# Output writes of a two-pair scan kernel, issued between the columns' steps, with the last two blocks written separately and the first pair's rows kept off a turn

## The chip, the cores and the metric

The kernel runs on one core of one Trainium2 chip. The metric is the device time of one execution in microseconds; the time of the kernel before is the median of three runs. The profile comes from one more execution, recorded by the hardware profiler, and its times count from the start of its span.

Engines are named as in the profile: PE is TensorE's matrix multiplication and PEld its weight load, DVE is VectorE, ACT is ScalarE, POOL is GpSimd, SP is the engine that issues nearly all the DMAs of this kernel (SPq in the profile). A line such as L1310 is a line of the kernel before.

## What is computed

The input is four images of 48 channels and 256 x 256 pixels in float32. Four layers follow one another, each as `x = x + layer(groupnorm(x))`. Layers 0 and 1 are an attention over channels and a gated convolution; the change does not touch them. Layers 2 and 3 are four scans each, and they fill most of the time:

```python
def step(w, b):                       # one row or column after the other
    def f(carry, inp):
        nxt = inp + _conv1d(carry, w, b)      # 48 -> 48 channels, 5 taps
        return (nxt, nxt)
    return f
# down over the rows, up over the rows, right over the columns, left over the columns
...
x = x + _L3_conv_ref(_gn(x), ...)
```

Every step needs the step before it, so a scan of 256 rows or columns is a chain of 256 convolutions.

## The kernel before

**Pairs and chains.** The four images are two pairs; a pair is one chain, `chain(pair)`, a Python generator that yields after every step of a row or column. In SBUF the 96 partitions hold 48 channels twice (even and odd positions), so the five taps become three matmuls of 96 x 96 by 128 (L1045, in `step`). Each step is done for the two images of the pair one after the other, called half steps below: three matmuls into PSUM, an addition on VectorE into one of four carry tiles (L1049 for the rows, L1053 for the columns), and `after`, which keeps the result: ScalarE's copy with the bias in the down, up and right scans (L1127, L1168, L1248), GpSimd's addition of the layer's input in the left scan (L1289, L1293).

**How the chains are interleaved.** The first chain gets a lead of `LEAD` = 992 steps. Then both chains step in turn, and TensorE has the other pair's matmuls to do while one pair waits for its addition. When the first chain has ended, the second runs its last 992 steps alone: the down, up, right and left scans of layer 3. During those, `to_rows(0)` brings the first pair's result, which lies column-wise in HBM, into the row order of the output: per piece four reads `oi<-x` (L1369) of 768 KB, eight copies in SBUF, six on GpSimd (L1383) and two on ScalarE (L1385), and two writes `out<-oo` (L1387) of 1536 KB. It is a generator of 24 pieces (eight times a set of reads and two halves), and the final loop takes one after every 28 steps.

**The left scan of the second pair** goes through 16 blocks of 16 columns, from n = 15 down to 0. At the first column of block n the loads for block n - 1 are issued on SP: `lines` (L1279), the right scan's result, and `stage` (L1280), the layer's input, 1536 KB each. Both come from a ring of five buffers of one block each, so `lines` takes the buffer of a `stage` used three blocks earlier, and `stage` that of a `lines` used two blocks earlier: it has to wait until VectorE has read the last column of that one. The second pair's result isn't written column-wise: GpSimd adds `stage` and the new carry straight into `done`, two tiles (one an image) that hold two blocks in row order, 32 columns. They come from the first pair's ring, which is otherwise used by then only for the rows of `to_rows`. After each even block four writes `out<-done` (L1310) go out, two images by two row parities, each of 768 KB in 6144 runs of 32 elements (128 B).

**The turn** is the change from the up scan to the right scan. The first block of columns (`col`) needs the first rows of the up scan (`col<-up`, L1180, and `col<-last`, L1192) directly out of SBUF; the second block is read from HBM (`col<-U`, L1235), after the last writes into `U` (L1200, L1207) have landed.

**What sets the order of the work.** Engines take their instructions in order. The order on each queue follows the order of emission only loosely: a scheduler at build time places each instruction by its own estimate of when its inputs and its buffer are ready, and adds the semaphore waits. In the order that results for the kernel before, SP has, for every two blocks of the left scan, the four writes, then `stage`, `lines`, `stage`, `lines`.

Of the kernel before, what the change touches and what calls it, by code (L numbers as in the profile page):

```python
# [16 lines left out]
B, C, H, W = 4, 48, 256, 256  # L17
# [97 lines left out]
def rows(pair):  # L115
    return slice(pair * P, (pair + 1) * P)
# [848 lines left out]
def scans(ctx, tc, xs, out, wts, biases, dram, k, coefs, lead, spare):  # L965
# [13 lines left out]
    nc = tc.nc  # L979
# [19 lines left out]
    CB = 2 * KC  # L999
# [12 lines left out]
    def take(pair, name):  # L1012
        return buffers[pair].tile([P, SLOT], F32, tag="slot", name=name)

    def chain(pair):
# [8 lines left out]
        def slot(name):  # L1024
            return take(pair, f"{name}{pair}")

        def inner():
            return carry[at[0]][:, :, 1 : HP - 1]
# [27 lines left out]
        def rows_view(t):  # L1056
            return t.rearrange("p (b k h w) -> p b k h w", b=2, k=NK, w=KC)

        def cols_view(t):
            return t.rearrange("p (b q h w) -> p b q h w", b=2, q=2, w=KC)  # L1060

        def lines_view(t):

            return t.rearrange("p (w b h) -> p w b h", w=CB, b=2)

        def row(ts, r):
            return rows_view(ts[r % 2])[:, :, :, r // 2, :]

        def load_rows(layer, n, ts, k0, k1):

            for r in range(2):
                v = rows_view(ts[r])
                for q in range(2):
                    for b in range(2):
                        nc.sync.dma_start(
                            v[q * C : (q + 1) * C, b, k0:k1].rearrange("c k h w -> c k (h w)"),
                            xs[layer][pair][
                                r * C : (r + 1) * C, b, 2 * k0 + q : 2 * k1 - 1 + q : 2, n * NH : (n + 1) * NH, :
                            ].rearrange("c k h w -> c k (h w)"),
                        )  # L1080

        def layer_of(layer, first):
# [32 lines left out]
            for n in range(NT):  # L1115
                ahead_ = None
                for r in range(RT):
# [3 lines left out]
                    if ahead_ and r >= RT // 2 and r % 4 == 0:  # L1121
                        i = (r - RT // 2) // 4
# [3 lines left out]
                    def keep(new, b):  # L1126
                        nc.scalar.activation(inp[:, b], blocks(new[:, b]), AF.Identity, bias=bias[:, 0:1])  # L1127
# [15 lines left out]
            for n in reversed(range(NT)):  # L1143
                ahead_ = None
                for r in reversed(range(RT)):
# [16 lines left out]
                    i = n * RT + r + 1  # L1162
                    if i == H:
                        continue
                    place = row(now, r)
# [4 lines left out]
                    if i == H - 1:  # L1170
                        keep(inner(), slice(0, 2))
                    else:
                        step(layer, 0, place, keep)
# [93 lines left out]
            following = None  # L1267


            direct = layer == 1 and pair == NP - 1  # L1270
            done = None
            for n in reversed(range(NK)):
                ahead_ = None
                if direct and n % 2 == 1:
                    done = [take(0, "done") for _ in range(2)]
                for w in reversed(range(CB)):
                    if w == CB - 1 and n > 0:
                        ahead_ = slot("lines"), slot("stage")
                        nc.sync.dma_start(ahead_[0], Rt[n - 1])  # L1279
                        nc.sync.dma_start(by_batch(ahead_[1]), block_of(x, n - 1))  # L1280
                    if layer == 0 and n == 0 and w == CB // 2:
                        following = [slot("dn"), slot("dn")]
                        load_rows(1, 0, following, 1, NK)
                    line = lines_view(lines)[:, w]
                    to = cols_view(stage)[:, :, w % 2, :, w // 2]

                    def keep(new, b):
                        if not direct:
                            nc.gpsimd.tensor_add(to[:, b], to[:, b], new[:, b])  # L1289
                            return  # L1290
                        for i in range(b.start, b.stop):
                            place = done[i].rearrange("p (h w) -> p h w", w=2 * CB)[:, :, n % 2 * CB + w]
                            nc.gpsimd.tensor_add(place, to[:, i], new[:, i])  # L1293

                    if n == NK - 1 and w == CB - 1:
                        keep(inner(), slice(0, 2))
                    else:
                        step(layer, 2, line, keep)
                    if late:
                        late.pop(0)()  # L1300
                    yield
                if not direct:
                    nc.sync.dma_start(block_of(y, n), by_batch(stage))
                elif n % 2 == 0:
                    for b in range(2):
                        at_rows = out[(2 * pair + b) * C : (2 * pair + b + 1) * C].rearrange(
                            "c (h r w) -> c h r w", r=2, w=W
                        )
                        for r in range(2):
                            nc.sync.dma_start(  # L1310
                                at_rows[:, :, r, n * CB : (n + 2) * CB],
                                done[b][r * C : (r + 1) * C].rearrange("c (h w) -> c h w", w=2 * CB),
                            )
                if layer == 0:

                    def stat(b, c, n=n, v=by_batch(stage)):
                        nc.vector.bn_stats(stats[b][:, n * 4 + c, :], v[:, b, c * 512 : (c + 1) * 512])

                    late += [lambda b=b, c=c, f=stat: f(b, c) for b in range(2) for c in range(4)]
                    if n == 0:  # L1320
                        for r in range(2):
                            for q in range(2):
                                nc.sync.dma_start(
                                    rows_view(following[r])[q * C : (q + 1) * C, :, 0].rearrange("c b h w -> c b (h w)"),
                                    cols_view(stage)[r * C : (r + 1) * C, :, q, :NH, :].rearrange("c b h w -> c b (h w)"),
                                )
                if ahead_:
                    lines, stage = ahead_
            if layer == 0:

                ends = []
                for b in range(2):
                    mv = work.tile([P, 2], F32, tag=f"mv{pair}{b}", name="mv")
                    late.append(
                        lambda b=b, mv=mv: nc.vector.bn_aggr(mv, stats[b].rearrange("p a b -> p (a b)"))
                    )
                    ends.append(k.group_norm_pieces(work, p_small, mv, "mean6", coefs[3][2 * pair + b], f"{pair}{b}"))
                for piece in late:
                    piece()
                    yield  # L1340
                for i in range(2):
                    for both in ends:
                        both[i]()
                    yield
                yield following
# [13 lines left out]
    def to_rows(pair):  # L1359

        y = xs[2][pair]
        nh = SLOT // W
        to = out[rows(pair)].rearrange("p (h w) -> p h w", w=W)
        for n in range(H // 2 // nh):
            got = []
            for r in range(2):
                t = take(pair, "oi")
                for b in range(2):
                    nc.sync.dma_start(  # L1369
                        t[b * C : (b + 1) * C].rearrange("c (k n) -> c k n", k=2 * NK),  # L1370
                        y[r * C : (r + 1) * C, b, :, n * nh : (n + 1) * nh, :].rearrange("c k h w -> c k (h w)"),
                    )
                got.append(t.rearrange("p (k q h w) -> p k q h w", k=NK, q=2, w=KC))
            yield
            for half in range(2):
                o = take(pair, "oo")
                v = o.rearrange("p (h r k w q) -> p h r k w q", h=nh // 2, r=2, k=NK, q=2)
                here = slice(half * nh // 2, (half + 1) * nh // 2)
                for i in range(4):
                    r, q = i // 2, i % 2  # L1380
                    dst, src = v[:, :, r, :, :, q], got[r][:, :, q, here, :].rearrange("p k h w -> p h k w")
                    if i < 3:
                        nc.gpsimd.tensor_copy(dst, src)  # L1383
                    else:
                        nc.scalar.copy(dst, src)  # L1385
                h0 = 2 * n * nh + half * nh
                nc.sync.dma_start(to[:, h0 : h0 + nh, :], o.rearrange("p (h w) -> p h w", w=W))  # L1387
                yield
# [9 lines left out]
        next(chains[1])  # L1398

    pieces = to_rows(0)  # L1400
    for i, _ in enumerate(chains[1]):
        if i % 28 == 27:
            next(pieces, None)
    assert next(pieces, True) is True

# [123 lines left out]
```

## Time and profile before

| What | Value |
|---|---|
| median of three runs (9152.1 to 9154.33) | 9154.29 us |
| the profiled execution, its own time | 9152.88 us |
| its span (first to last instruction) | 9151.1 us |
| mean granted TensorE clock | 0.979 |
| busy: PE, PEld, DVE, ACT, POOL | 95%, 80%, 41%, 38%, 23% |
| DMA, whole span | 152 GB/s mean, 1390.61 MB |
| chain by engine | PE 89%, DMA 4%, DVE 3%, ACT 2% |
| second chain alone: down and up scans | about 7555 to 8309 us |
| its right scan, from the turn | 8309 to 8667 us |
| its left scan; writes of its output | from 8667; first write issued at 8729.85 |
| last addition on VectorE; end of the last write's packets | 9120.9; 9149.5 us |

How to read it: the chain of waits goes back from the last instruction, at each step to what released it. A piece named PE there is time in which TensorE set the pace; a piece named DMA is time in which an engine waited for a transfer. An SPq line is the issue of a DMA on SP, with the time it held SP; the landing comes later. In the view by windows, "DMA share" is the mean busy share of the core's sixteen DMA engines (packets that overlap can bring it above 1), and PEclk is the granted clock. The view of the DMA queues gives for a window, behind each queue, its packets, its MB, and the time its packets took as a share of sixteen engines' time in the window.

### The profile page before, as it was taken

What the parts mean: (1) busy time and instruction counts of PE and PEld (TensorE: products, weight loads), DVE (VectorE), ACT (ScalarE), POOL (GpSimd) and SP (SyncE); (2) the same over time, 40 slices, a digit from 0 to 9 for tenths busy, and PEclk for the clock granted to TensorE, in tenths of its full rate; (3) what the DMA queues carried; (4) which work ended last, traced back from release to release, by engine and by line L of the source; (5) the groups of instructions that cost most, each with busy time, mean ns of one, the idle gap of its engine ahead of it and who ended that gap; (6) DMA issues with size and microseconds to landing.
All of it is one profiled execution on the core that took longest, in us unless ns stands there. A gap on an engine that the chain in (4) does not pass through costs nothing.

```text
span 9151.1 us, 162340 instructions
## 1 busy us (share of the span) xinstructions
PE 8728.1 (95%) x62920; PEld 7283.8 (80%) x62920; DVE 3763.0 (41%) x10790; ACT 3489.5 (38%) x7033; POOL 2073.9 (23%) x3855
## 2 busy tenths in 40 slices
PE   6999999999999887999999999999999999999986
PEld 4777777433333346999999999999999999998986
DVE  3232010234555564444455444444445554343432
ACT  0001000123343356755502766665661006665500
POOL 0000000001111120002464000003446772003464
PEclk9999999999999988999999999999999999999998
DMA  7663323468788868665587773656556787888677
GB/s 149 133 132 87 73 63 72 95 138 175 173 182 181 174 156 178 130 141 138 142 218 172 146 159 92 153 130 169 145 161 186 218 220 158 180 183 203 172 153 146
DMA packets 1177350, 1390.61 MB, mean 152 GB/s; under 512 B 261072, under 2 KB 1103568, under 8 KB 1113600
## 3 DMA queue, kind: packets, MB, share of 16 engines
q1 hardware_dynamic: 1176480, 1379.90, 66.5%
q8 instruction: 493, 8.08, 0.4%
q14 instruction: 281, 2.30, 0.1%
q0 software_dynamic: 96, 0.33, 0.0%
HBM read 812.02 MB, written 509.61 MB: 144 GB/s over the span
## 4 chain that ended last, share of the span: by engine, by line
PE 89%; DMA 4%; DVE 3%; ACT 2%; issue 1%; SPq 1%; POOL 1%; DVEq 0%; POOLq 0%; ACTq 0%
PE ps L1045 58%; PE py L581 7%; PE acc L294 5%; PE acc L295 5%; PE acc L296 4%; PE py L590 4%; PE pt L276 1%; DMA stage<-x 1%; DMA tok<-x 1%; PE ph L698 1%; ACT x1n L541 1%; PE pout L868 1%; PE ptok L751 1%; DMA x<-y 1%; DMA sx<-in_x 1%
## 5 line engine op out<-in xcount | busy, mean ns | idle before, releaser
L1045 PE MATMUL ps<-carry,w 96*96 96x128 f32 x48960 | 5505.8, 275 | 135.9 <-DVE carry L1053 89.3
L1045 PEld LDWEIGHTS ps<-carry,w 96*96 96x96 f32 x48960 | 5456.1, 163 | 188.9 <-DVE carry L1053 100.5
L1225 POOL COPY pre<-col 96x256 f32<-96x256 f32 x1020 | 656.7, 645 | 2737.5 <-DMA col<-last 1948.3
L1248 ACT ACTIVATE lines<-carry,b 96x128 f32<-96x128 f32 (+1 forms) x2044 | 816.9, 402 | 623.6 <-DVE carry L1053 614.5
L1127 ACT ACTIVATE dn<-carry,b 96x128 f32<-96x128 f32 (+1 forms) x2044 | 770.5, 398 | 715.0 <-DVE carry L1049 712.1
L1049 DVE TENSOR_TENSOR carry<-ps,dn 96x128 f32<-96x128 f32 x2280 | 655.2, 288 | 892.9 <-PE ps L1045 803.3
L1053 DVE TENSOR_TENSOR carry<-ps,pre 96x128 f32<-96x128 f32 x2040 | 587.2, 288 | 796.8 <-PE ps L1045 544.0
L1168 ACT ACTIVATE up<-carry,b 96x128 f32<-96x128 f32 x1792 | 718.3, 402 | 481.6 <-DVE carry L1049 480.6
L1053 DVE TENSOR_TENSOR carry<-ps,lines 96x128 f32<-96x128 f32 x2040 | 577.0, 286 | 741.4 <-PE ps L1045 645.4
L1289 POOL TENSOR_TENSOR stage<-stage,carry 96x128 f32<-96x128 f32 (+1 forms) x1533 | 793.1, 521 | 312.3 <-DVE carry L1053 184.2
L1049 DVE TENSOR_TENSOR carry<-ps,up 96x128 f32<-96x128 f32 x1792 | 516.4, 288 | 678.3 <-PE ps L1045 668.9
L581 PE MATMUL py<-x1n,wy 128*96 128x512 f32 x1536 | 700.8, 605 | 30.2 <-ACT x1n L541 27.9
L294 PE MATMUL acc<-xt 128*96 128x288 f32 x2048 | 666.9, 409 | 0.0
L295 PE MATMUL acc<-xs,xt 128*96 128x288 f32 x2048 | 666.9, 407 | 0.0
L581 PEld LDWEIGHTS py<-x1n,wy 128*96 128x96 f32 x1536 | 244.0, 165 | 452.4 <-issue 435.0
L261 ACT ACTIVATE xn<-raw,coef 96x2048 f32<-96x2048 f32 x64 | 133.6, 2094 | 986.9 <-PE pt L276 819.8
L296 PE MATMUL acc<-xt,xs 128*96 128x192 f32 x2048 | 501.7, 327 | 0.0
L279 DVE COPY xt<-pt 128x384 f32<-128x384 f32 x256 | 136.6, 554 | 851.5 <-PE pt L276 650.6
L296 PEld LDWEIGHTS acc<-xt,xs 128*96 128x96 f32 x2048 | 332.2, 165 | 154.4 <-issue 1.5
L295 PEld LDWEIGHTS acc<-xs,xt 128*96 128x96 f32 x2048 | 332.1, 164 | 151.2 <-issue 2.4
L604 DVE TENSOR_TENSOR y<-py,t 96x512 f32<-96x512 f32 x256 | 171.4, 677 | 592.1 <-PE py L590 586.2
L590 PE MATMUL py<-x2n,wy 64*96 64x512 f32 x1536 | 363.0, 601 | 0.0
(179 smaller groups left out, 4843.4 us busy)
## 6 DMA issues: line engine op xcount, KB each, us to landing
stage<-x SPq DMA_DIRECT2D x64, 1536.0 KB
dn<-x SPq DMA_DIRECT2D x240, 384.0 KB
col<-U SPq DMA_DIRECT2D x60, 1536.0 KB
R<-lines SPq DMA_DIRECT2D x60, 1536.0 KB
lines<-R SPq DMA_DIRECT2D x60, 1536.0 KB
D<-dn SPq DMA_DIRECT2D x56, 1536.0 KB
up<-D SPq DMA_DIRECT2D x56, 1536.0 KB
U<-up SPq DMA_DIRECT2D x224, 384.0 KB
```

The costliest lines, as they stand in the source:

```text
L294: nc.tensor.matmul(acc[0], lhsT=xt[:, h + 2, :], rhs=xt[:, here, :], start=first, stop=last)
L295: nc.tensor.matmul(acc[1], lhsT=xt[:, h + 2, :], rhs=xs[:, here, :], start=first, stop=last)
L296: nc.tensor.matmul(acc[2], lhsT=xs[:, h + 2, :], rhs=xt[:, past, :], start=first, stop=last)
L581: nc.tensor.matmul(ps, lhsT=held["w"][0][:, dx], rhs=x1n[:, 2 * c : 2 * c + 2, dx : dx + W], start=dx == 0, stop=False)
L590: nc.tensor.matmul(held["ps"][q + 2 * s], lhsT=held["w"][1][here, dx], rhs=x2n[here, 2 * q : 2 * q + 2, dx : dx + W], start=False, stop=dx ...
L1045: nc.tensor.matmul(ps, lhsT=w_sb[layer][:, way, j, :], rhs=old[:, i, j : j + W // 2], start=j == 0, stop=j == 2)
L1049: nc.vector.tensor_add(new[:, i].rearrange("p (k w) -> p k w", w=KC), ps.rearrange("p (k w) -> p k w", w=KC), inp[:, i])
L1053: nc.vector.tensor_add(new[:, i], ps, inp[:, i])
L1127: nc.scalar.activation(inp[:, b], blocks(new[:, b]), AF.Identity, bias=bias[:, 0:1])
L1168: nc.scalar.activation(place[:, b], blocks(new[:, b]), AF.Identity, bias=bias[:, 1:2])
L1248: nc.scalar.activation(line[:, b], new[:, b], AF.Identity, bias=bias[:, 2:3])
L1289: nc.gpsimd.tensor_add(to[:, b], to[:, b], new[:, b])
```

## The change

The change is in `layer_of` (the left scan of the last layer of the second pair) and in the last loop of `scans`. It has three parts.

1. The four writes of a block pair are no longer issued together. They go into a list, and one is taken out after the steps with `w % 8 == 4`, which is two a block (in the last two blocks after every fourth step, four a block). What is left in the list when the scan ends is issued then.
2. Blocks 1 and 0 are written separately. Their `done` is one tile for both images with 16 columns, so each gives four writes of 6144 runs of 16 elements (64 B) and 384 KB, in place of four writes of 128 B runs for both blocks.
3. The pieces of `to_rows(0)` come after fixed steps: sixteen from step 20 on, every 26 steps (to 410), and eight from step 508 on, every 28 (to 704). None lies between 410 and 508. The up scan ends at about step 480.

The computation itself and all other DMAs are the same. In the order that the scheduler gives to SP now, each block of the left scan has `lines`, `stage`, write, write (the first pair of writes has `stage` between them); after the last `stage` come the last four writes of 128 B runs, then the eight of 64 B runs.

```diff
             direct = layer == 1 and pair == NP - 1
-            done = None
+            done, width = None, 0
+            writes = []
             for n in reversed(range(NK)):
                 ahead_ = None
-                if direct and n % 2 == 1:
-                    done = [take(0, "done") for _ in range(2)]
+                if direct and n < 2:
+                    done, width = take(0, "done").rearrange("p (b n) -> b p n", b=2), CB
+                elif direct and n % 2 == 1:
+                    done, width = [take(0, "done") for _ in range(2)], 2 * CB
...
-                            place = done[i].rearrange("p (h w) -> p h w", w=2 * CB)[:, :, n % 2 * CB + w]
+                            place = done[i].rearrange("p (h w) -> p h w", w=width)[:, :, n * CB % width + w]
                             nc.gpsimd.tensor_add(place, to[:, i], new[:, i])
...
                     if late:
                         late.pop(0)()
+                    if writes and (w % 4 == 0 if n < 2 else w % 8 == 4):
+                        writes.pop(0)()
                     yield
                 if not direct:
                     nc.sync.dma_start(block_of(y, n), by_batch(stage))
-                elif n % 2 == 0:
-                    for b in range(2):
+                elif n * CB % width == 0:
+
+                    def write(b, r, done=done, width=width, w0=n * CB):
                         at_rows = out[(2 * pair + b) * C : (2 * pair + b + 1) * C].rearrange(
                             "c (h r w) -> c h r w", r=2, w=W
                         )
-                        for r in range(2):
-                            nc.sync.dma_start(
-                                at_rows[:, :, r, n * CB : (n + 2) * CB],
-                                done[b][r * C : (r + 1) * C].rearrange("c (h w) -> c h w", w=2 * CB),
-                            )
+                        nc.sync.dma_start(
+                            at_rows[:, :, r, w0 : w0 + width],
+                            done[b][r * C : (r + 1) * C].rearrange("c (h w) -> c h w", w=width),
+                        )
+
+                    writes += [lambda b=b, r=r, f=write: f(b, r) for b in range(2) for r in range(2)]
...
+            for write in writes:
+                write()
...
     pieces = to_rows(0)
+    times = [20 + 26 * i for i in range(16)] + [508 + 28 * i for i in range(8)]
     for i, _ in enumerate(chains[1]):
-        if i % 28 == 27:
+        if i in times:
             next(pieces, None)
```

## The prediction

> **What bounds the kernel now.** I read the page first (chain by line, tenths of the span), then the chain of waits in order of time for the last 400 us, the SP queue's own timeline there, and the DMA view of short windows. The page says TensorE is busy 95% of the span and makes 89% of the chain; what the change touches is the rest. The last pass of the second pair runs from 8667 us, and from 8730 us its output is written. The chain there:
>
> ```profile
> 8739.93 10.68 PE ps L1045 x96
> 8750.61 15.71 DMA stage<-x
> ...
> 8766.45 0.53 POOL done L1293
> ...
> 8767.34 40.46 PE ps L1045 x332
> 8807.80 15.19 DMA stage<-x
> ```
>
> A load of `stage` ends the wait, 15 us long, and again 57 us later; seven such pieces lie before the end. GpSimd (L1293) waits for the load, VectorE and TensorE for GpSimd through the four carry tiles. Why the load is late is on SP:
>
> ```profile
> 8729.85 20.66 SPq L1310 DMA_DIRECT2D out<-done  x4
> 8750.61 5.51 SPq L1280 DMA_DIRECT2D stage<-x  x1
> 8756.16 0.59 SPq L1279 DMA_DIRECT2D lines<-R  x1
> 8756.85 0.56 SPq L1280 DMA_DIRECT2D stage<-x  x1
> 8757.51 0.56 SPq L1279 DMA_DIRECT2D lines<-R  x1
> ```
>
> Four output writes go out back to back at the end of a block pair and hold SP 20.66 us, then hold up the next issue 5.51 more; the loads for two blocks stand behind them. A block is 16 columns of 1.345 us (VectorE's additions in the timeline, at full clock), 21.5 us, so the stage load comes out just when it is needed. But how much is there to win? The stretches between two late loads:
>
> ```profile
> core 0: us, PE busy (x) PEld busy (x) DVE busy (x) ACT busy (x) POOL busy (x), PEclk, DMA share, GB/s
> 8807.80:8862.53 54.73, 44.37 (x378) 44.05 (x377) 18.05 (x63) 0.00 (x0) 31.93 (x64) 0.91 0.89 173
> 8862.53:8918.05 55.52, 45.55 (x391) 45.21 (x390) 18.73 (x65) 0.00 (x0) 33.09 (x66) 0.91 0.88 171
> ```
>
> A block pair takes 55 to 57 us where the columns need 43, and the DMA share is already 0.88. The queue is badly ordered, and it is also nearly full. The three lines below are the DMA view of 8756 to 8786 (the four loads), 8727 to 8757 (the four writes) and 8336 to 8337 (the tiny `U<-last` writes of 32 B runs at the turn):
>
> ```profile
> q1 hardware_dynamic: 1381, 6.38, 94.3%
> ...
> q1 hardware_dynamic: 24648, 3.21, 75.0%
> ...
> q1 hardware_dynamic: 1348, 0.06, 74.3%
> ```
>
> Loads: 0.943 x 30 = 28.3 us of sixteen engines, 7.07 each. Writes: 0.75 x 30 = 22.5 us, 5.62 each, 14.6 ns a packet on one engine (0.75 x 30 x 16 / 24648). Tiny packets: 8.8 ns (0.743 x 16 / 1348 us).
>
> **What the Trainium skill says.** "Perfetto Trace Analysis", DMA Instruction — HWDGE: the slice of a DMA on its issuing engine is descriptor generation, not movement, and the next instruction stands behind it. The trace agrees: the write's cost shows on SP, and partly in the following load's 5.51 us. "DMA: Bandwidth & Descriptors", Queues, rings and completion order: descriptors of one engine's ring are consumed in order. It agrees too: after 8756 us 6.38 MB of loads move in one run, behind the writes. The same page, Specifications: under 512 B a transfer doesn't reach line rate, because of a read-modify-write; Why small descriptors are slow: a fixed overhead per packet. The trace has both sides: 128 B packets at 14.6 ns, tiny ones at 8.8, so the cost falls far less than the bytes.
>
> **The change part by part.** (1) *Writes one by one.* No packet is removed. In the changed kernel's instruction order SP has, for each block, `lines`, `stage`, write, write, in place of four writes and then two of each load, so a stage load has at most the previous block's two writes ahead of it, and no more the whole four. The `done` wait stays on GpSimd and is long met. What queues behind a write on SP now is the next block's pair of loads. Would the old 15 us wait vanish? TensorE runs on about 6 us past a block's end before it stops (8751.4 to 8757), so the load may be 6 us late for nothing. What is late next is the DMA queue itself: a block brings 2 x 7.07 + 2 x 5.62 = 25.4 us of packets against 21.5 us of columns. So I cost this stretch as DMA-bound: from the first write's packets at 8731 us there are 25 loads (13 of `stage`, 12 of `lines`) and 28 writes, 25 x 7.07 + 28 x 5.62 = 334.2 us, to 9065.2. The last stage load ends four writes earlier, at 9042.7, lands about 2 us later; less 6 us of slack the last block begins about 9039 and computing ends at 9060 (now 9121.6). TensorE then loses 9060 - 8730 - 14 x 21.5 = 29 us instead of 91.
>
> Bounds of this: shares above 1 occur where many transfers overlap (1.06 in the loads' 5 us windows), 334.2 / 1.06 = 315, 19 us less. Upwards, elapsed time: the four writes took 26.3 us from 8730.5 with dips between them (6.6 each), the loads 27 (6.75 each): 25 x 6.75 + 28 x 6.6 = 353.6, 19 us more. Loads queued ahead should fill part of the dips, so I take 334.
>
> (2) *The last two blocks by themselves.* The last pair's four writes become eight of as many packets (6144) at 64 B. No row of before shows 64 B. Lower end the tiny packets, 8.8 ns x 384 per engine = 3.4 us; upper end 128 B, 5.6 us; I take the middle, 4.5, an estimate from those two rows. Eight take 36 us, four of them under block 0, where no load is left to be delayed. They cannot start before the 9065 of the earlier writes, so the queue sets the end: 9065.2 + 36 + 1.6 (from the last packets at 9149.5 to the end of the span now) = 9102.8. That is 48 us under the span of 9151.1. Eight at 3.4 or 5.6 make it 9 less or more. The GpSimd additions keep their count and shape (0.52 us against 0.67 us for a half step): nothing.
>
> (3) *No rows near the turn.* The turn, up to right, loses much: 8309.4 to 8389.2 us has 457 matmuls, at the later 8.73 per us 52 us of work in 80. Its chain:
>
> ```profile
> 8310.14 1.09 ACT oo L1385
> ...
> 8314.66 5.04 DMA col<-last
> ...
> 8339.72 15.34 DMA col<-U
> ...
> 8383.83 1.12 POOL oo L1383
> ```
>
> Only little is the rows' doing: ScalarE's copy and the write behind it (8310.1 to 8311.7) hold two `col<-up` issues that were ready, about 2.5 us; and 1.5 MB of rows (`out<-oo`, issued 8337.5) lie ahead of `col<-U`, about 5.5 us. In the new order ScalarE's copies and both writes stand before the turn, but one 0.77 MB read of rows (7.07 / 2 = 3.5 us) still stands ahead of `col<-U`, and two GpSimd copies (1.1 us each) now come into the first block after it, where the 6 us hold-up at 8383 moves to. The rest, the writes of U that must land, stays. Saving 2.5 + 2 less a little: 4 us, between 0 and 8. The earlier rows come every 26 steps instead of 28; ScalarE's order in the down pass, where the waits are its normalizations (6 us a block), keeps its sequence. I take 0.
>
> Sum: 48 + 4 = 52. The profiled execution took 9152.88 (span 9151.1 and 1.8 around it), the median is 9154.29, 1.4 above; 9154.3 - 52 = 9102.
>
> **The rivals.** (a) *The columns set the pace.* If loads and writes mixed overlap better than they did in a row, a block fits into 21.5 us: computing ends at 8730 + 301 = 9031, then four 64 B writes, 18 us, and 3 around them: 9052, 99 us less, and the turn: 9051. For it: whole 50 us windows show a DMA share of 1.17 (7800 to 7850, other shapes). Against: 25.4 must shrink by 15%, and the writes alone never moved above about 147 GB/s. (b) *The dips stay.* A write behind full rings holds SP, so the next loads come out only when the second write is handed over; `R<-lines` at 8345 was held 12.05 us in that way behind a read of rows. Then elapsed times count: 8731 + 353.6 + 8 x 6.2 + 1.6 = 9136, 15 less, with the turn 9135. (c) *The 64 B packets are dear*, a slower kernel: their place is the end, after 9065, with nothing to hide them. It decides from (9151.1 - 1.6 + 4 - 9065.2) / 8 = 11 us a write, 29 ns a packet, twice the 128 B price; at 15 us the end is 9065.2 + 120 + 1.6 = 9187, 36 later, 9186 with the turn. For it: the read-modify-write that the skill names; against: the tiny packets' 8.8 ns, also into HBM.
>
> **How the numbers follow.** DMA-bound 0.70 (9102, own range 9074 to 9124: 19 and 9 down, and 8 to 19 up); columns 0.11 (9051); dips stay 0.15 (9135); dear packets 0.04 (9186). The range 9074 to 9130 leaves out (a), (c) and the upper part of (b), some 0.2. About 0.2% (18 us) is what a measurement of this kernel tells from no change: faster takes 0.70, 0.11 and 0.10 of (b), 0.91; the same, 0.05; slower 0.04.
>
> **What would show it.** On SP, two writes and two loads in turn from 8730, no run of four until the end; stage waits of 2 to 5 us a block after the first three instead of 15 a pair; DMA share near 1 there; computing ending near 9060, the tail some 40 us with eight 64 B writes of about 4.5. Share below 0.9 with waits left means (b), no waits means (a), a tail beyond 90 us means (c). I am wrong elsewhere if the down pass or the turn shifts by over 10 us.

## The result, and the profile after

| | us |
|---|---|
| before, median of 4 runs | 9153.19 (9148.12 to 9154.33) |
| after, median of 4 runs | 9100.12 (9095.42 to 9107.06) |
| ratio | 0.9942, 95% interval 0.9926 to 0.9958 |
| the profiled execution of after | 9095.42, its span 9093.6 |

The change saves some 53 us, and the forecast was 9102. The two spans lie 57.5 us apart. Cut at the same four instructions, the two traces show where that is:

| stretch | before | after | gained |
|---|---|---|---|
| up to the down scan of the second pair's last layer (nothing in it is changed) | 7555.1 | 7551.7 | 3.4 |
| down and up scans | 719.1 | 726.4 | -7.3 |
| turn and right scan, up to the first output write on SP | 455.6 | 449.1 | 6.5 |
| left scan, from that write to the end of the span | 421.25 | 366.4 | 54.9 |

The first line is what two executions differ by anyway: over the ten profiled executions of this document that stretch took 7550.2 to 7559.4 us. The last line is the change's aim; the two between cancel.

**The left scan.** The SP queue's timeline of after, two stretches of it (start, duration, issue):

```profile
8795.02 0.58 SPq L1284 DMA_DIRECT2D stage<-x  x1
8795.65 17.41 SPq L1316 DMA_DIRECT2D out<-done  x2
8813.16 5.59 SPq L1283 DMA_DIRECT2D lines<-R  x1
8818.84 0.58 SPq L1284 DMA_DIRECT2D stage<-x  x1
...
9014.15 0.58 SPq L1284 DMA_DIRECT2D stage<-x  x1
9014.82 71.32 SPq L1316 DMA_DIRECT2D out<-done  x12
```

Two writes and one `lines` load now stand between two `stage` issues; the groups of four are gone. At the end stand twelve writes together: four of 128 B runs and all eight of 64 B runs. From the issue at 8771.09 to that at 9014.15 are ten blocks, 24.3 us each. The columns need 21.5, so something still waits. The chain of waits of after, its pieces in the last 500 us:

```profile
8599.86 267.49 PE ps L1045 x2370
...
8867.35 15.94 DMA stage<-x
...
8884.33 6.95 PE ps L1045 x60
...
8891.67 15.95 DMA stage<-x
...
9008.67 15.55 DMA lines<-R
...
9024.69 22.98 PE ps L1045 x174
```

From 8599.86 the chain is TensorE alone for 267 us, almost six blocks of writing among them; the first late `stage` ends a wait at 8883.3, where before it was at 8766.3. A DMA piece of 16 us is a load's whole way and not the time that an engine stood. That is in GpSimd's waits from 8700 us on (total, times, longest):

```profile
POOL done L1297 <- DMA stage<-x: 46.3, 8, 7.6
```

Before it was 105.6 us in 7 waits, the longest 15.9. Now the DMA queue itself is the limit. The first two lines below are blocks with no wait yet, the third has one, the last is the tail after the last matmuls (a half step, three matmuls in the program, is six records of PE in these counts):

```profile
core 0: us, PE busy (x) PEld busy (x) DVE busy (x) ACT busy (x) POOL busy (x), PEclk, DMA share, GB/s
8795.02:8818.84 23.82, 23.82 (x215) 23.74 (x214) 10.20 (x36) 0.00 (x0) 18.29 (x37) 1.00 1.10 201
8818.84:8843.00 24.16, 24.16 (x218) 24.11 (x217) 10.37 (x36) 0.00 (x0) 18.63 (x37) 1.00 1.04 196
8989.10:9014.15 25.05, 22.51 (x200) 21.97 (x199) 9.43 (x33) 0.00 (x0) 16.21 (x34) 1.00 1.04 190
9048.10:9093.60 45.50, 0.24 (x3) 0.02 (x1) 0.29 (x1) 0.00 (x0) 1.04 (x2) 0.52 0.98 83
```

The share is above 1 in each of the ten blocks (1.03 to 1.10), and in the first of them TensorE is still full: the loads' issues fall behind by 24.3 - 21.5 = 2.8 us a block, at first unseen, since a load comes out a block ahead of its use. The DMA view of the ten blocks and of 9053 to 9092 (packets, MB, share of 16 engines):

```profile
q1 hardware_dynamic: 126367, 47.18, 105.2%
...
q1 hardware_dynamic: 48747, 3.11, 102.3%
```

47.18 MB in 243 us is 194 GB/s, against 171 to 173 in block pairs before. The second line is the 64 B writes: 1.023 x 39 x 16 / 48747 = 13.1 ns a packet, and 39 / 8 = 4.9 us a write.

A wait costs TensorE more than the time in which it stands. The granted clock in three stretches of after, around the last late load, a `lines` that landed at 9024.2 (columns as above):

```profile
9022.00:9024.00 2.00, 0.91 (x9) 0.69 (x7) 0.00 (x0) 0.00 (x0) 0.52 (x1) 1.00 0.97 213
...
9026.00:9028.00 2.00, 2.00 (x12) 1.99 (x11) 0.54 (x2) 0.00 (x0) 0.00 (x0) 0.52 1.02 238
...
9034.00:9036.00 2.00, 2.00 (x20) 1.99 (x19) 0.86 (x3) 0.00 (x0) 1.90 (x5) 1.00 1.00 138
```

TensorE stands for about 2 us, and then the clock is at 0.50 to 0.52 from 9026 to 9032, with 11 or 12 records in 2 us instead of 20. From the first output write to the end of computing PE is busy 319.6 us before and 311.1 after for the same 2685 records; in the run with half of the writes, further down, where the clock stays at 1.00, it is 301.1. So by these figures the lower clock cost some 18 us before and 10 after, beside 72 and 10 us of standing still.

**The down scan**, where 7 us were lost. After's chain there:

```profile
7821.62 39.83 PE ps L1045 x354
...
7864.83 10.73 DMA dn<-x
```

A load of the down pass ends an idle time that before has not. Its issue on SP, before and then after:

```profile
7824.66 22.86 SPq L1075 DMA_DIRECT2D dn<-x  x8
7849.40 0.35 SPq L1387 DMA_DIRECT2D out<-oo  x1
```

```profile
7845.85 0.33 SPq L1397 DMA_DIRECT2D out<-oo  x1
7846.23 0.42 SPq L1136 DMA_DIRECT2D D<-dn  x1
7846.74 22.87 SPq L1075 DMA_DIRECT2D dn<-x  x8
```

With the pieces 26 steps apart a rows write stands ahead of the eight `dn` loads. SP waits 27.2 us there for ScalarE's copies into the write's tile (L1395 of after), and the loads come out 22 us later (7846.74 against 7824.66). The loads themselves are no slower: SP is on them for 22.9 us in both.

### The profile page after: what moved, and what is told of

Its sections match the earlier page's. It is cut to its first block, busy times and chain, and to the rows that moved or that the text cites. A ratio compares the mean times of both kernels' runs of the same rounds, so it can differ in the third digit from the quotient of the medians.

```text
span 9093.6 us, 162344 instructions
## 1 busy us (share of the span) xinstructions
PE 8711.1 (96%) x62920; PEld 7268.3 (80%) x62920; DVE 3759.8 (41%) x10790; ACT 3489.6 (38%) x7033; POOL 2067.0 (23%) x3855
## 4 chain that ended last, share of the span: by engine, by line
PE 88%; DMA 4%; DVE 3%; ACT 1%; issue 1%; SPq 1%; POOL 1%; DVEq 0%; POOLq 0%; ACTq 0%
PE ps L1045 57%; PE py L581 7%; PE acc L294 6%; PE acc L295 5%; PE acc L296 4%; PE py L590 3%; PE pt L276 1%; DMA stage<-x 1%; DMA tok<-x 1%; PE ph L698 1%; PE pout L868 1%; DMA x<-y 1%; PE ptok L751 1%; ACT x1n L541 1%; DMA sx<-in_x 1%
```

## The experiments

Theory: in the left scan the sum of the DMA packets sets the end once SP's order no longer does; the split of the last blocks costs packets at a place where nothing hides them. Rivals: SP's being held by writes is what still counts; the split or the piece steps carry part of the gain. The first four kernels take the parts separately.

**Part 1 alone**: writes one by one, all of 128 B runs, pieces every 28 steps as before. Against the changed kernel:

```diff
-                if direct and n < 2:
-                    done, width = take(0, "done").rearrange("p (b n) -> b p n", b=2), CB
-                elif direct and n % 2 == 1:
+                if direct and n % 2 == 1:
...
-    times = [20 + 26 * i for i in range(16)] + [508 + 28 * i for i in range(8)]
+    times = [27 + 28 * i for i in range(24)]
```

> The writes one by one, alone: 128 B runs to the end, the rows' pieces at their old steps. Theory (the sixteen DMA engines set the pace, so the end is the sum of their packets): the block pace is that of the changed kernel, 24.3 us, and the end is earlier than its by the eight 64 B writes (4.9 us each) less four of 128 B (5.6 each), 16 us; the rows' shift nets to nothing. So about 9084 us. Rival (the split blocks are what shortens the end, since half of their writes lie under the last block): slower than the changed kernel by the four large writes, some 10 us, about 9110.

Measured: 9081.07 (9075.6 to 9086.22), before in the same runs 9148.22; ratio 0.9928 (0.9914 to 0.9941). Left scan 351.0 us, down and up scans 719.0, turn and right scan 455.1. So part 1 by itself does all of the gain, its left scan is 15 us shorter than that of the whole change, and its down scan has no loss. SP at its end:

```profile
9017.82 0.58 SPq L1282 DMA_DIRECT2D stage<-x  x1
9018.50 58.21 SPq L1314 DMA_DIRECT2D out<-done  x8
```

Eight writes instead of twelve follow the last load, in 58 us instead of 71.

**Part 2 alone**: the split, writes issued at once, pieces as before. Against the changed kernel:

```diff
-                    if writes and (w % 4 == 0 if n < 2 else w % 8 == 4):
-                        writes.pop(0)()
...
-                    writes += [lambda b=b, r=r, f=write: f(b, r) for b in range(2) for r in range(2)]
+                    for b in range(2):
+                        for r in range(2):
+                            write(b, r)
...
-    times = [20 + 26 * i for i in range(16)] + [508 + 28 * i for i in range(8)]
+    times = [27 + 28 * i for i in range(24)]
```

> The last two blocks by themselves, alone: four 64 B writes issued together after block 1 and four after block 0, all else as before. Here the DMA queue is empty under the last block (idle from 9103 to 9121 in the profile of before), so four of the eight writes are hidden there. Theory: the end after computing falls from 29.5 us to 4 x 4.9 + 3 = 23, so 7 us less, about 9146. Rival (64 B writes are as dear in total as 128 B ones of twice the bytes, or dearer): 9153 or above.

Measured: 9142.51 over 13 runs; ratio 0.9995 (0.9987 to 1.0004), which can't be told from no change. Its left scan took 412.5 us in the profiled execution, 8.8 less than before. The split is no loss by itself, and the trace shows why:

```profile
9079.44 5.44 SPq L1284 DMA_DIRECT2D stage<-x  x1
9084.98 43.00 SPq L1314 DMA_DIRECT2D out<-done  x8
```

The first four 64 B writes move nearly whole between 9094 and 9112 us (22509 of 24576 packets), under the columns of block 0; in the kernel before the DMA share is 0.00 there (9103 to 9121). Only the other four are left when computing ends, and the span ends 22.2 us after the last addition on the chain instead of 30.2.

**Part 3 alone**: the kernel before, with the new piece steps.

```diff
     pieces = to_rows(0)
+    times = [20 + 26 * i for i in range(16)] + [508 + 28 * i for i in range(8)]
     for i, _ in enumerate(chains[1]):
-        if i % 28 == 27:
+        if i in times:
```

> The rows' pieces at the new steps, alone. Theory: 6.5 us gained at the turn, 7.3 us lost in the down and up scans where a load of dn came late, as in the trace of the changed kernel; within 5 us of 9153. Rival (the loss in the down scan belongs to one execution, not to the spacing): 9147.

Measured: 9150.25 over 21 runs; ratio 1.0004 (0.9997 to 1.001). Zero, made of two things: the turn and right scan took 451.6 us (4.0 less than before), the down and up scans 725.6 (6.5 more). The late load is in its chain too, though the left scan is untouched:

```profile
7824.24 39.84 PE ps L1045 x354
...
7867.62 10.82 DMA dn<-x
```

**The changed kernel without the split** (parts 1 and 3). Against it:

```diff
-                if direct and n < 2:
-                    done, width = take(0, "done").rearrange("p (b n) -> b p n", b=2), CB
-                elif direct and n % 2 == 1:
+                if direct and n % 2 == 1:
```

> The changed kernel without its second part: one by one, new steps for the rows, 128 B runs to the end. Theory (DMA engines' sum): 16 us under the changed kernel, about 9084. Rival (the split shortens the end): about 9110.

Measured: 9089.07 (9077.92 to 9090.85); ratio 0.9935 (0.9922 to 0.9947). Left scan 352.3 us, against 366.4 with the split (365.1 in a second profile of the changed kernel): here the split costs 13 to 14 us. Some 11 of them lie behind the end of computing (from the last addition on the chain to the end of the span, 34.2 us against 45.5): with the split the queue still has all eight 64 B writes to move then, 39 us, and without it the four of 128 B runs and what is left of the four ahead of them. The other 3 us are lost before computing ends. The whole times do not show the split by themselves: 0.9935 against 0.9942 for the change, with intervals that overlap. The profiled execution reached the down scan at 7559.1 us, 7.4 later than that of the changed kernel, in a part where nothing differs.

The second four ask whether SP or the packets set the pace, and whether the two losses can be left off.

**The writes on ScalarE's queue.**

```diff
-                        nc.sync.dma_start(
+                        nc.scalar.dma_start(
                             at_rows[:, :, r, w0 : w0 + width],
```

> The changed kernel with its output writes issued on ScalarE's queue, which has no work in this scan; loads stay on SP, so no load stands behind a write any more on its issuing engine. Theory (the sixteen DMA engines set the pace): the same packets, so the block pace stays at 24 us or a little more, the DMA share above 1, and the time within 8 us of the changed kernel's. Rival (SP, held 18 us by two writes and then 5.4 by the load behind them, 24.1 of each 24.3 us, sets the pace): blocks of 21.5 to 22 us, ten to twelve of them 2.5 us shorter, and 25 to 30 us less.

Measured: 9102.74 (9100.32 to 9104.1); ratio 0.9949 (0.9936 to 0.9963). The changed kernel in the same runs had 9094.21 (9091.17 to 9100.09). The time came as expected, no gain (if anything a loss of 8 us), but one thing that I had written was wrong: the pace of the blocks did not stay at 24 us. Three successive `stage` issues on SP, 21.5 us apart, which is the columns' own pace, and the writes on ScalarE's queue:

```profile
8733.67 0.55 SPq L1284 DMA_DIRECT2D stage<-x  x1
...
8755.20 0.55 SPq L1284 DMA_DIRECT2D stage<-x  x1
...
8776.74 0.55 SPq L1284 DMA_DIRECT2D stage<-x  x1
```

```profile
8733.61 360.16 ACTq L1316 DMA_DIRECT2D out<-done  x36
```

No wait for `stage` is left. The loads pass the writes, the writes pile up, and the wait comes back for a free `done` tile (GpSimd's waits):

```profile
POOL done L1297 <- DMA out<-done: 19.6, 2, 19.2
```

Six blocks run at full pace at a share of 1.04, then computing stops for the writes; the share is 1.01 from there until computing ends at 9057, and the same eight 64 B writes follow:

```profile
core 0: us, PE busy (x) PEld busy (x) DVE busy (x) ACT busy (x) POOL busy (x), PEclk, DMA share, GB/s
8733.67:8862.86 129.19, 129.19 (x1155) 128.70 (x1153) 55.35 (x192) 0.00 (x0) 99.80 (x192) 1.00 1.04 202
...
9057.00:9101.60 44.60, 0.00 (x0) 0.00 (x0) 0.07 (x1) 0.00 (x0) 0.52 (x1) 0.53 0.97 81
```

Left scan 367.9 us from the first write's issue, against 366.4. The queue decides which transfer is late, not when the last one is done. That rules out SP's holding as the limit of the changed kernel. "DMA: Bandwidth & Descriptors" of the Trainium skill, Issuing engines are not separate DMA queues, says that DMAs from several engines run on the same 16 DMA engines and that issuing on more than one saves sequencer time only; the equal end agrees, but the order among transfers did change.

**Half of the writes left out.** The writes of the odd rows of blocks 15 to 2 are not made, so that part of the output is missing; everything is computed.

```diff
-                    writes += [lambda b=b, r=r, f=write: f(b, r) for b in range(2) for r in range(2)]
+                    writes += [lambda b=b, r=r, f=write: f(b, r) for b in range(2) for r in range(1 if n > 1 else 2)]
```

> The changed kernel that leaves out the writes of the odd rows of blocks 15 to 2 (fourteen of its thirty-six writes), so these rows of the output are missing. What a block brings is then 2 x 7.07 + 5.62 = 19.8 us of packets, less than the 21.5 us of its columns. Theory: no wait for stage is left, computing ends 14 x 21.5 us after the first write, and the end follows by four 64 B writes and 3 us, 23 us: 42 us less than the changed kernel, about 9057. If the waits stayed with a DMA share well under 1, something other than the packets would set the pace.

Measured: 9055.06 (9054.57 to 9064.4); ratio 0.99 (0.9887 to 0.9914). This takes away half of SP's holding as well as half of the 128 B packets, so it does not tell the two apart; the run before does. With the packets fewer, no wait for a load is left and the columns set the pace:

```profile
core 0: us, PE busy (x) PEld busy (x) DVE busy (x) ACT busy (x) POOL busy (x), PEclk, DMA share, GB/s
8772.95:9031.00 258.05, 257.96 (x2301) 256.10 (x2299) 110.40 (x383) 0.00 (x0) 199.67 (x384) 1.00 0.91 172
9031.00:9052.80 21.80, 0.00 (x0) 0.00 (x0) 0.29 (x1) 0.00 (x0) 0.74 (x2) 0.54 1.09 75
```

It ends computing at 9031 and needs 21.8 us more. This is the floor that rival (a) described; the changed kernel, which must move all packets, lies 41 us above it in spans (9093.6 against 9052.8).

**One by one, no split, pieces every 28 steps with the gap only.** Against the changed kernel without the split:

```diff
-    times = [20 + 26 * i for i in range(16)] + [508 + 28 * i for i in range(8)]
+    times = [27 + 28 * i for i in range(15)] + [508 + 28 * i for i in range(9)]
```

> One by one, no split, and the rows' pieces every 28 steps from 27 to 419 as before, then none until 508. Theory (the wait for dn in the down scan comes from the 26-step spacing alone): its 7 us are not there, the 4 to 6.5 us at the turn stay: about 9078, 5 us under the kernel with the first part alone. Rival (any piece moved before the turn is only traded for another wait): no less than 9082.

Measured: 9074.34 (9067.43 to 9081.12); ratio 0.9919 (0.9906 to 0.9931). Down and up scans 718.9 us, turn and right scan 450.0, left scan 351.75: both losses are off and the turn's gain is kept. In the same runs the changed kernel had 9094.21, ratio 0.9941 (0.9929 to 0.9954), 20 us more; by stretches 366.4 - 351.75 = 14.6 and 726.4 - 718.9 = 7.5 of it. It has the lowest median of the versions here that write everything; that it beats part 1 alone (0.9928, 0.9914 to 0.9941) is not clear of the noise.

## Why the prediction was right, point by point

- *Writes one by one, DMA-bound.* Right in mechanism. The order on SP is two writes and two loads in turn, the share is near 1 (1.03 to 1.10), and the experiments with fewer writes and with another queue show that the packets set the end. Size: 334 us were forecast for 25 loads and 28 writes; the first 64 B packet moves at about 9053, 325 us after the first write. 25.4 us of packets a block went through in 24.3, a share of 1.05. I had bounded the overlap at 1.06 and taken none. Computing ended at 9048 (forecast 9060), and TensorE lost 9048 - 8727 - 14 x 21.5 = 20 us instead of 29 (91 before). The forecast had no term of its own for the clock: half of the 20 us, and a fifth of the 91, is work at the lower clock after a wait.
- *Stage waits of 2 to 5 us after the first three blocks.* The waits came later and were longer: none for almost six blocks, then 8 waits of 5.8 us on average, up to 7.6, on GpSimd.
- *The last two blocks by themselves.* "I take the middle, 4.5": it was 4.9, so the tail after the 128 B writes took 40.6 us (9093.6 - 9053) instead of 37.6. "Four of them under block 0" failed: when computing ends at 9048 the queue is still on 128 B writes, and all eight 64 B writes come after it. The sum was not hurt, since it set the eight behind the queue and took nothing off for those four. What I had not worked out is that the split is a loss of 14 us in this company: alone it gives 8.8 us in the profile. The reason is the room in the queue under block 0: before, nothing moved there from 9103 to 9121, and with the split alone four of the eight writes move in it. One by one, the queue is full until the end, and twice as many packets at nearly the same price each lengthen it.
- Left scan in all: 48 forecast, 54.9 measured: 9 more from the overlap, 3 less from the 64 B writes.
- *No rows near the turn.* 4 us forecast, between 0 and 8. The turn and right scan gained 6.5 in the changed kernel, 4.0 with part 3 alone, and 5.6 with the gap only (455.6 to 450.0). Right in the sum, not in its terms: from the end of the up scan to the first matmuls of the columns the chain took 11.4 us before and 4.0 after, 7.3 less where I had 2.5 (`col<-last` ends its wait after 1.6 us instead of 5.0); the wait for `col<-U` fell from 15.3 to 14.2, 1.1 where I had 2; and of these 8.4 us 6.5 are left at the first output write.
- *"The earlier rows come every 26 steps instead of 28; ScalarE's order in the down pass keeps its sequence. I take 0."* This step failed. I had looked at ScalarE and not at SP, where the rows write is moved past the `dn` loads: 7.3 us lost, and 6.5 with part 3 alone. It stays within the 10 us beyond which I had called myself wrong, and it took away the gain of the turn, so the total did not show it. That 52 was forecast and 53 measured is thus in part luck; the sum is closer than its terms: 7 us too few in the left scan, 7 too many in the down pass, and what the turn gave beyond 4 is of the size by which two executions differ.
- *Rivals.* (a) needed a block in 21.5 us; it took 24.3. The ScalarE queue run reached 21.5 for six blocks, by leaving writes behind, and ended no earlier. (b), dips: the share was never below 1.03 in the ten blocks. Two writes hold SP for 17.41 us, and the next issue shows 5.59; that a DMA's slice on its issuing engine is not its movement (the Trainium skill, "Perfetto Trace Analysis", DMA Instruction — HWDGE) agrees with this, since the sixteen engines stayed full meanwhile. (c), 64 B at 11 us a write: 4.9.

Left open: why mixed loads and writes overlap to 1.05, which no run isolates; why the clock falls after some waits and not after others; and the 9 us over which executions differ before the second pair's last layer begins, which limit each comparison of whole times.

## What to carry to other kernels

When the DMA engines' packets fill a stretch, the order of issues only decides which transfer is late: on one queue the loads, on two the writes, and the end hardly moves. Order pays up to that point (here the share in the left scan rose from 0.88 to 1.05); beyond it, count packets. An edit that was a gain or free because a queue stood idle under it (the split) can stop being free when another edit fills that time, so parts must be judged together. A DMA moved by a few steps is also moved past others on its in-order queue: look there at who now stands behind it and what it waits for, even where the engine's own work keeps its order.

## What the runs showed of the hardware

- With nothing but writes on the queue, a write of 6144 packets of 64 B took 4.9 us (384 KB, 80 GB/s; the changed kernel, 9053 to 9092), and one of as many packets of 128 B took 6.4 us (768 KB, 122 GB/s; part 1 alone, 29556 packets in the 31 us from 9051 on, share 0.83). Half the bytes saved a quarter of the time. By the busy share, a packet took one engine 13.1 ns at 64 B in the changed kernel and 14.4 to 15.1 with the split alone, against 14.0 to 14.6 at 128 B: little or nothing less. I had expected the middle between 14.6 and 8.8.
- Loads and 128 B writes mixed moved at 190 to 202 GB/s at a share of 1.03 to 1.10.
- Writes on a second engine's queue let the loads pass them: blocks at 21.5 us instead of 24.3, and a wait of 19.2 us for a `done` tile in its place.
- After waits in the left scan TensorE's granted clock was 0.50 to 0.52 for some microseconds (9026 to 9032 in after, 8760 to 8772 before), and working at it, PE did 11 or 12 records in 2 us instead of 20; over the scan this cost some 18 us before and 10 after.
